# Two attention layers: phases of one and a half key tiles in place of steps of one

## The chip, the cores and the metric

The kernel runs on one core of a Trainium2 chip. The core has TensorE (PE), VectorE (DVE), ScalarE (ACT), GpSimd (POOL) and SyncE (SP); each takes its instructions in the order in which they were written, and semaphores hold an instruction back until what it needs is done. TensorE writes to PSUM, which has eight banks, each of 512 floats on 128 partitions; ScalarE and VectorE read it. The metric is the time of one execution on the device in microseconds (us); the median of several runs counts.

## The reference

Two layers, each normalizing an image of 4 x 256 x 64 x 64 floats by groups (_gn) and adding attention to it:

```python
q = jnp.einsum('oc,bchw->bohw', Wq, x).reshape(b, nh, hd, h * w)          # layer 0: 4096 queries,
k = lax.conv_general_dilated(x, Wk, window_strides=(SR, SR), ...)          # 1024 keys of a strided conv
attn = jnp.einsum('bhdn,bhdm->bhnm', q, k) + jnp.einsum('bhdn,hdm->bhnm', q, pos)
out = jnp.einsum('bhdm,bhnm->bhdn', v, jax.nn.softmax(attn * scale, axis=-1))

attn = jax.nn.softmax(jnp.einsum('bihd,bjhd->bhij', q, k) * scale, axis=-1) # layer 1: four areas of 1024 tokens
out = jnp.einsum('bhij,bjhd->bihd', attn, v) + _dwconv7(v_full, w_pe, b_pe)
return _conv1x1(out, w_proj, b_proj)
```

There are 8 heads of 32 channels; every query meets 1024 keys in either layer. All is float32.

## The kernel before

Work is cut into 8 blocks (layer A or B, image b), each of 16 units. A unit is 512 queries of four heads (one half of the channels), and has 8 key tiles of 128 keys: 1024 steps of one key tile in all. The main loop at the end of direct_path writes one step per pass, and the instruction order of all five engines is just the order of that writing (manual_schedule); no scheduler moves anything.

A step does the following.

- scores (L267): four products, one for each head, 32 channels deep, each in its own row tile of TensorE, into two pairs of PSUM banks (ps_pair, tag "s", three pairs that take turns). The first pair holds heads 0 and 1, the second heads 2 and 3.
- Two exponentials on ScalarE (L271), one for each pair, from PSUM into tiles p in SBUF (tag "p", ten buffers of 128 x 1024).
- weighted (L278): the values times the weights of the step before, four products, each in its own column tile, accumulated over the unit in the one bank av. At a unit's first step the finished av is copied to av_sb by ScalarE (L886), between the two exponentials.
- VectorE adds the p of each step to the first one of the unit (L865), one step later.
- do(g, j): whatever plan has for this step: loads, norms (ScalarE, L249), statistics, additions, transposes.
- Up to three parts of side tasks: the queue side holds the projections for q, k and v of later units, the output projections (product, L158) and the 7 x 7 convolution (L800). A part is four to eight products in column tiles. Most tasks have two parts, k and v of layer A four. A task's result lies in the one bank "side", from where ScalarE or VectorE moves it on.

Three steps after a unit's end come divisors (L288: ones times the summed weights, four products, in a pair of the tag "s") and divide: ScalarE copies the sums to den_sb (L305), POOL's queue takes them through DRAM to a narrow layout; five steps later reciprocals (L313) and their way back (L315, L317) to the tile rb, and five steps after that multiply (L320). So the PSUM banks are six for scores and divisors, one av, one side.

In the profile every float32 product appears as two matmuls, and a weight load (PEld) for each.

## Time and profile before

| What | us |
|---|---|
| median of 3 runs (3207.05 to 3210.25) | 3207.16 |
| span of the profiled execution | 3201.2 |
| scores, L267, busy, two blocks of layers | 601.5 + 593.8 |
| weighted sums, L278, busy | 552.5 + 545.2 |
| divisors, L288, busy | 142.4 |
| first score product starts at | 82.74 |
| last group of scores of the main loop starts at | 3174.61 |
| idle TensorE before a score product, all in all | 0.8 |

A line of groups has the source line, engine, operation, the tile written and those read, the shape and the count; then busy time, the mean of one in ns, and the idle time of the engine before them with what ended it. Matmuls overlap, and their ends are modelled; the starts are the better measure.

### The profile page before, as it was taken

Reading aid. Unit: us, or ns where it says so; the run is one execution under the profiler, and the core shown is the slowest. Engines: PE = TensorE matmul, PEld = TensorE weight load, DVE = VectorE, ACT = ScalarE, POOL = GpSimd, SP = SyncE. Lnnn points to the kernel's source line nnn. Section 1 sums busy time; section 2 is a strip of 40 time slices with the busy share of each in tenths; the row PEclk is TensorE's granted clock in tenths of the full one; section 3 lists DMA queues with packets and bytes.
Section 4 is the critical chain, followed back from the end, with each engine's and each line's share of the span. In section 5 each row is a group of like instructions: output and inputs, shape, how many; then the busy total and the mean of one; then the engine's idle time right before and its main releaser. Section 6 shows DMA issues by size and latency. Waiting matters only on the chain.

```text
span 3201.2 us, 75820 instructions
## 1 busy us (share of the span) xinstructions
PE 3159.5 (99%) x30762; PEld 960.0 (30%) x30762; DVE 2506.7 (78%) x2719; ACT 2520.7 (79%) x2988; POOL 487.7 (15%) x923
## 2 busy tenths in 40 slices
PE   7999999999999999999999999999999999999998
PEld 4233323332233332323223322323233333222222
DVE  3787897778887777877777777777788788888888
ACT  2888888887887878888887777777777777788876
POOL 0111121111211111111111111111111111111111
PEclk9999999999999999999999999999999999999999
DMA  5242343454545456777776666676555655423222
GB/s 183 43 104 74 92 105 85 95 125 108 129 111 140 125 135 173 163 175 177 198 175 161 182 174 158 169 176 161 155 143 144 167 151 149 128 72 80 70 51 59
DMA packets 648191, 421.53 MB, mean 132 GB/s; under 512 B 411773, under 2 KB 556637, under 8 KB 647833
## 3 DMA queue, kind: packets, MB, share of 16 engines
q1 hardware_dynamic: 619384, 380.11, 46.6%
q0 software_dynamic: 28448, 36.48, 4.6%
q8 instruction: 245, 4.01, 0.5%
q14 instruction: 114, 0.93, 0.1%
HBM read 318.32 MB, written 98.09 MB: 130 GB/s over the span
## 4 chain that ended last, share of the span: by engine, by line
PE 93%; issue 2%; DVE 2%; DMA 1%; ACT 1%; SPq 1%; POOL 0%; DVEq 0%; ACTq 0%; POOLq 0%
PE s L267 33%; PE av L278 29%; PE den L288 4%; PE k0ps L158 4%; PE q0ps L158 3%; PE k1ps L158 3%; PE q1ps L158 3%; PE v0ps L158 3%; PE conv_ps L800 3%; PE vals_ps L158 3%; PE ops L158 3%; DVE p L865 1%; ACT p L271 1%; DMA first<-in_x 0%; DMA share<-vals 0%
## 5 line engine op out<-in xcount | busy, mean ns | idle before, releaser
L865 DVE TENSOR_TENSOR p<-p 128x1024 f32<-128x1024 f32 x1790 | 2108.3, 1219 | 505.4 <-ACT p L271 454.9
L271 ACT ACTIVATE p<-s 128x1024 f32<-128x1024 f32 x2048 | 2016.6, 1026 | 512.7 <-PE s L267 497.3
L267 PE MATMUL s<-q,k_A 32*128 32x512 f32 x4096 | 601.5, 640 | 0.5 <-ACT p L271 0.3
L267 PE MATMUL s<-q,k_B 32*128 32x512 f32 x4096 | 593.8, 640 | 0.3 <-ACT p L271 0.3
L278 PE MATMUL av<-p,v_A 128*32 128x512 f32 x4096 | 552.5, 604 | 0.0
L278 PE MATMUL av<-p,v_B 128*32 128x512 f32 x4096 | 545.2, 603 | 0.0
L317 POOL DMA_DIRECT2D rb<-recs x508 | 252.0, 501 | 490.4 <-DMA recs<-few 414.5
L267 PEld LDWEIGHTS s<-q,k_B 32*128 32x128 f32 x4096 | 165.3, 182 | 384.5 <-issue 294.8
L267 PEld LDWEIGHTS s<-q,k_A 32*128 32x128 f32 x4096 | 172.8, 183 | 330.7 <-issue 253.1
L315 POOL DMA_DIRECT2D recs<-few x127 | 70.1, 552 | 1283.7 <-DVE sums L314 1208.4
L278 PEld LDWEIGHTS av<-p,v_A 128*32 128x32 f32 x4096 | 89.1, 108 | 381.2 <-issue 333.6
L278 PEld LDWEIGHTS av<-p,v_B 128*32 128x32 f32 x4096 | 87.6, 108 | 378.8 <-issue 335.2
L288 PE MATMUL den<-p,ones 128*32 128x512 f32 x1032 | 142.4, 606 | 3.1 <-DVE p L865 3.1
L307 POOL DMA_DIRECT2D few<-rows x127 | 72.3, 569 | 454.6 <-DMA rows<-den_sb 447.2
L158 PE MATMUL ops<-cv,wp_sb 128*32 128x512 f32 x1024 | 131.7, 593 | 4.4 <-DVE cv L577 3.0
L158 PE MATMUL k0ps<-taps,wkv 128*32 128x256 f32 x2048 | 130.2, 386 | 2.5 <-ACT taps L249 2.5
L158 PE MATMUL q1ps<-h,wqkv_sb 128*32 128x512 f32 x1024 | 131.5, 592 | 0.0
L158 PE MATMUL vals_ps<-hv,wqkv_sb 128*32 128x512 f32 x1024 | 129.9, 592 | 0.0
L306 POOL DMA_DIRECT2D rows<-den_sb x127 | 74.4, 586 | 363.6 <-ACT den_sb L305 358.6
L158 PE MATMUL k1ps<-h,wqkv_sb 128*32 128x512 f32 x1024 | 128.7, 592 | 0.2 <-ACT cout L811 0.2
L158 PE MATMUL q0ps<-hq,wq_sb 128*32 128x512 f32 x1024 | 128.2, 592 | 0.0
L158 PE MATMUL v0ps<-wkv,taps 128*32 128x256 f32 x2048 | 126.0, 379 | 0.3 <-ACT v_A L400 0.3
(90 smaller groups left out, 1686.3 us busy)
## 6 DMA issues: line engine op xcount, KB each, us to landing
rows<-vals SPq DMA_DIRECT2D x384, 195.9 KB
rb<-recs POOLq DMA_DIRECT2D x508, 64.0 KB, 3.3
share<-vals SPq DMA_DIRECT2D x128, 195.9 KB
vala<-vout SPq DMA_DIRECT2D x128, 144.0 KB
vals<-vout SPq DMA_DIRECT2D x128, 144.0 KB
vc<-vala SPq DMA_DIRECT2D x64, 288.0 KB
band<-mats SPq DMA_DIRECT2D x96, 176.0 KB
hq<-in_x SPq DMA_DIRECT2D x32, 512.0 KB
```

What stands on the lines that cost most here:

```text
L158: T.matmul(out[cols, :], lhsT=lhsT[:, cols], rhs=rhs, start=start, stop=stop)
L267: T.matmul(pairs[h // 2][:, h % 2, :], lhsT=k[rows, unit[0], j * P : (j + 1) * P], rhs=q[rows, :], start=True, stop=True,)
L271: exps = [lambda i=i: S.activation(p[i], pairs[i], AF.Exp, scale=SCALE) for i in range(2)]
L278: T.matmul(av[HD * h : HD * h + HD, :], lhsT=v[:, j, unit[0] * P + HD * h : unit[0] * P + HD * h + HD], rhs=p[h // 2][:, h % 2, :], start= ...
L288: T.matmul(dens[g][HD * h : HD * h + HD, :], lhsT=ones, rhs=p[h // 2][:, h % 2, :], start=(n == 0), stop=(n == len(ps) - 1),)
L306: G.dma_start(rows, den_sb[0:P:HD, :])
L307: G.dma_start(few[:, 0, :], rows.rearrange("h (q n) -> (h q) n", n=CH // HD))
L315: G.dma_start(recs.rearrange("h (q n) -> (h q) n", n=CH // HD), few[:, 1, :])
L317: G.dma_start(rb[HD * h : HD * h + HD, :], recs[h : h + 1, :].to_broadcast([HD, CH]))
L800: T.matmul(ps[HD * m : HD * m + HD, (2 * k + i) * size : (2 * k + i + 1) * size].rearrange("p (y x) -> p y x", y=NY), lhsT=band[:, half].r ...
L865: soon(1, lambda i=i: V.tensor_add(ps[0][i], ps[0][i], ps[j][i]))
```

## The change

A pass of the loop now is a phase of one and a half key tiles (683 phases for 1024 tiles). parts_of says which: an even phase has a whole key tile and the first half (256 queries) of the next one, an odd phase the second half and the whole tile after that. The scores of a phase fill all six banks: a has heads 0 and 2 of the whole tile, b heads 1 and 3, c the four halves, two to a bank. The halves of heads 1 and 3 go first, then the whole products of 0, 2, 1, 3, then, behind a fence, the halves of 0 and 2. In the next phase b and c have changed places. There are three exponentials in a phase, and the weighted sums of the phase before follow: four products of 512 columns and four of 256.

The weights of a unit are summed in a tile of their own, acc (two buffers of 128 x 2048): the first key tile's exponentials write it, the others are added to it. The buffers of tag "p" become six. den, and the two small products of a norm, move from the score banks to the side bank.

In the loop, when a unit ends inside a phase (cut), its last weighted sums come first, av is copied to av_sb between the second and the third exponential, and the new unit's weighted sums come last. Between the two stand either the divisors of a finished unit or up to two parts of one side task. After the weighted sums come further parts: up to four of one task if divisors were written, up to two if the task has more than two parts or more than seven parts wait. reciprocals stands at step 0 of the second unit on, four steps ahead of multiply.

```diff
-    first = [pool.tile([P, CT, CH], FP, tag="p", name=f"first_{c}", bufs=10) for c in range(NCH)]
+    first = [pool.tile([P, CT, CH], FP, tag="p", name=f"first_{c}", bufs=PB) for c in range(PB)]
+    rest_of_first = pool.tile([P, 4, CH], FP, tag="acc", name="first", bufs=2)
+    first += [rest_of_first[:, :2, :], rest_of_first[:, 2:, :]]
...
+    def ps_banks(n, name):
+        return psum.tile([P, 2, CH], FP, tag=f"s{n}", name=name, bufs=1)
+
+    turn = [0]
+
     def ps_pair(name):
-        return psum.tile([P, 2, CH], FP, tag="s", name=name, bufs=3)
+        turn[0] += 1
+        return ps_banks(turn[0] % 3, name)
...
-            ps = ps_pair(f"gm_{name}")[:, 0, :CT]
+            ps = ps_side(f"gm_{name}")[:, :CT]
...
+    HC = CH // 2
+    accs, made_p = {}, {}
+    in_bank, bank_count = tc.alloc_semaphore("in_bank"), [0]
+
+    def acc_of(g):
+        if g not in accs:
+            accs[g] = pool.tile([P, 4, CH], FP, tag="acc", name="acc", bufs=2)
+        return accs[g]
+
+    def pair_of(h):
+        return slice(2 * (h % 2), 2 * (h % 2) + 2)
+
+    def acc_half(g, u):
+        return acc_of(g).rearrange("p (l b) (u n) -> p u b l n", l=2, u=2)[:, u]
+
+    def parts_of(f):
+
+        full, half = (3 * f + 1) // 2, (3 * f // 2 + 1, 0) if f % 2 == 0 else (3 * f // 2, 1)
+        return (full if full < last else None), (half if half[0] < last else None)
+
+    def score_product(out, s, h, cols):
+        g, j = divmod(s, NKT)
+        rows, unit = slice(HD * h, HD * h + HD), units[g]
+        return T.matmul(
+            out, lhsT=unit[2]()[rows, unit[0], j * P : (j + 1) * P], rhs=unit[1]()[rows, cols], start=True, stop=True
+        )
+
+    def scores(f):
+
+        full, half = parts_of(f)
+        a, b, c = [ps_banks(n, "s") for n in ((0, 1, 2) if f % 2 == 0 else (0, 2, 1))]
+        every = slice(0, CH)
+
+        def half_product(h):
+
+            u = half[1]
+            return score_product(
+                c[:, h // 2, HC * (h % 2) : HC * (h % 2) + HC], half[0], h, slice(HC * u, HC * u + HC)
+            )
+
+        if half is not None:
+            for h in (1, 3):
+                first = half_product(h).then_inc(in_bank, 1)
+                tc.add_to_no_dep_group(f"first_{f}", first.ins)
+                tc.no_tile_sem_insts.add(first.ins.name)
+                bank_count[0] += 1
+        for h in (0, 2, 1, 3):
+            score_product((a, b)[h % 2][:, h // 2, :], full, h, every)
+        if half is not None:
+            fence = T.wait_ge(in_bank, bank_count[0])
+            tc.declare_fence(fence.ins, group=f"first_{f}")
+            for h in (0, 2):
+                half_product(h)
+
+        def exp_full(n):
+            g, j = divmod(full, NKT)
+            if j == 0:
+                p = acc_of(g)[:, pair_of(n), :]
+            else:
+                p = pool.tile([P, 2, CH], FP, tag="p", name="p", bufs=PB)
+            made_p[full, n] = p
+            S.activation(p, (a, b)[n], AF.Exp, scale=SCALE)
+
+        def exp_half():
+            if half is None:
+                return
+            (g, j), u = divmod(half[0], NKT), half[1]
+            if j == 0:
+                p = acc_half(g, u)
+            else:
+                p = pool.tile([P, 2, CH], FP, tag="p", name="p", bufs=PB).rearrange("p b (l n) -> p b l n", l=2)
+            made_p[half[0], 2 + u] = p
+            S.activation(p, c.rearrange("p b (l n) -> p b l n", l=2), AF.Exp, scale=SCALE)
+
+        return [lambda: exp_full(0), lambda: exp_full(1), exp_half]
+
+    def weighted(s, av, u=None):
+
+        g, j = divmod(s, NKT)
+        unit, v = units[g], units[g][3]()
         for h in range(4):
-            rows = slice(HD * h, HD * h + HD)
+            if u is None:
+                out, rhs = av[HD * h : HD * h + HD, :], made_p[s, h % 2][:, h // 2, :]
+            else:
+                out = av[HD * h : HD * h + HD, HC * u : HC * u + HC]
+                rhs = made_p[s, 2 + u][:, h // 2, h % 2, :]
             T.matmul(
-                pairs[h // 2][:, h % 2, :], lhsT=k[rows, unit[0], j * P : (j + 1) * P], rhs=q[rows, :],
-                start=True, stop=True,
+                out, lhsT=v[:, j, unit[0] * P + HD * h : unit[0] * P + HD * h + HD], rhs=rhs,
+                start=(j == 0 and not u), stop=(j == NKT - 1), skip_group_check=True,
             )
-        exps = [lambda i=i: S.activation(p[i], pairs[i], AF.Exp, scale=SCALE) for i in range(2)]
-        return p, exps
-
-    def weighted(unit, j, p, av):
-
-        v = unit[3]()
-        for h in range(4):
-            T.matmul(
-                av[HD * h : HD * h + HD, :], lhsT=v[:, j, unit[0] * P + HD * h : unit[0] * P + HD * h + HD],
-                rhs=p[h // 2][:, h % 2, :], start=(j == 0), stop=(j == NKT - 1),
-            )
-
-    def divisors(g, *ps):
-
-        dens[g] = ps_pair("den")[:, 0, :]
-        for n, p in enumerate(ps):
+
+    def add_up(s, n):
+
+        g = s // NKT
+        p, acc = made_p[s, n], acc_of(g)
+        to = acc[:, pair_of(n), :] if n < 2 else acc_half(g, n - 2)
+        V.tensor_add(to, to, p)
+
+    def divisors(g, *extra):
+
+        dens[g] = ps_side("den") if g < len(units) - 1 else ps_pair("den")[:, 0, :]
+        acc = accs.pop(g)
+        sets = [lambda h: acc[:, 2 * (h % 2) + h // 2, :]] + [lambda h: made_p[s, h % 2][:, h // 2, :] for s in extra]
+        for n, p in enumerate(sets):
             for h in range(4):
                 T.matmul(
-                    dens[g][HD * h : HD * h + HD, :], lhsT=ones, rhs=p[h // 2][:, h % 2, :],
-                    start=(n == 0), stop=(n == len(ps) - 1),
+                    dens[g][HD * h : HD * h + HD, :], lhsT=ones, rhs=p(h),
+                    start=(n == 0), stop=(n == len(sets) - 1),
                 )
 
     def divide(g, unit):
 
         if g == len(units) - 1:
 
-            rb = pool.tile([P, CH], FP, tag="p", name="rb", bufs=10)
+            rb = pool.tile([P, CH], FP, tag="p", name="rb", bufs=PB)
             V.reciprocal(rb, dens[g])
             V.tensor_mul(unit[4]()[:, unit[0], :], avs.pop(g), rb)
             spare.extend((dens.pop(g), rb))
@@ -319,7 +409,7 @@
         def multiply():
             V.tensor_mul(unit[4]()[:, unit[0], :], avs.pop(g), made["rb"])
 
-        at(g + 1, 7 if g < len(units) - 2 else 4, reciprocals)
+        at(*((g + 2, 0) if g < len(units) - 2 else (g + 1, 6)), reciprocals)
         at(g + 2, 4 if g < len(units) - 2 else 0, multiply)
...
+    final = len(units) - 1
+    av_of, weights_left, sums_left, opened = {}, {}, {}, set()
+    to_add, to_divide = deque(), deque()
+
+    def accumulate(s, u):
+
+        g = s // NKT
+        if g not in weights_left:
+            av_of[g] = psum.tile([P, CH], FP, tag="av", name="av", bufs=1)
+            weights_left[g] = 2 * NKT
+        weighted(s, av_of[g], u)
+        weights_left[g] -= 2 if u is None else 1
+        if weights_left[g] <= 2 * (NKT - 1):
+            opened.add(g)
+
+    def evict(g):
+        if weights_left[g] == 0 and g in av_of:
+            avs[g] = pool.tile([P, CH], FP, tag="av", name="av_sb", bufs=2)
+            S.copy(avs[g], av_of.pop(g))
+
+    def add_ready():
+
+        for _ in range(len(to_add)):
+            s, n = to_add.popleft()
+            g = s // NKT
+            if s % NKT and g not in opened:
+                to_add.append((s, n))
+                continue
+            if s % NKT and s != last - 1:
+                add_up(s, n)
+            sums_left[g] = sums_left.get(g, 2 * NKT) - 1
+            if sums_left[g] == 0:
+                to_divide.append(g)
+
+    def side_parts(budget):
+
+        mine, done = side[0] if side else None, 0
+        while done < budget and side and side[0] is mine:
+            advance()
+            done += 1
+
+    f = step = 0
+    before = []
+    while f < PHASES or before or plan or side or to_add or to_divide:
+        now[0] = step
+        exps = scores(f) if f < PHASES else [lambda: None] * 3
+        exps[0]()
+        due = bool(to_divide)
+        add_ready()
+        due = bool(to_divide) if f >= PHASES else due
+        cut = next((n for n in range(1, len(before)) if before[n][0] // NKT != before[0][0] // NKT), 0)
+        for s, u in before[:cut]:
+            accumulate(s, u)
+        exps[1]()
+        if cut:
+            evict(before[0][0] // NKT)
+        exps[2]()
+        while step < -(-3 * (f + 1) // 2):
+            do(*divmod(step, NKT))
+            step += 1
         waiting = sum(n for n, _ in side)
-        for n in range((waiting > 0) + (waiting > 7) + (waiting > 14) - (j == 2)):
-            if n and side[0] is not task_now:
-                break
-            task_now = side[0]
-            advance()
-            if not side:
-                break
-        before = None
-        if now[0] < last:
-            if j == 0:
-                av = psum.tile([P, CH], FP, tag="av", name="av", bufs=1)
-            sum_up(g, j, ps)
-            before = units[g], j, ps[j], av
-        now[0] += 1
+        whole = side[0][0] if side else 0
+        if due:
+            g = to_divide.popleft()
+            divisors(g, *([last - 1] if g == final else []))
+            if g < final:
+                divide(g, units[g])
+        else:
+            side_parts(2)
+        for s, u in before[cut:]:
+            accumulate(s, u)
+        add_ready()
+        if due:
+            side_parts(4)
+        elif whole > 2 or waiting > 7:
+            side_parts(2)
+        if before:
+            evict(before[-1][0] // NKT)
+        before = []
+        if f < PHASES:
+            full, half = parts_of(f)
+            before = sorted(([half] if half else []) + [(full, None)], key=lambda b: b[0])
+            to_add.extend((s, n) for s, u in before for n in ((0, 1) if u is None else (2 + u,)))
+        f += 1
```

More of the change, by code (lines that the diff above doesn't have):

```diff
@@ L47 @@
 LIMIT = 1e25
+PB = 6
 BLOCKS = [("A", b) for b in range(B)] + [("B", b) for b in range(B)]
 UNITS = 2 * NCH
+PHASES = -(-2 * len(BLOCKS) * UNITS * NKT // 3)
 @with_exitstack
@@ L229, in variances @@
         def variances():
-            ps = ps_pair(f"gv_{name}")[:, 0, :CT]
+            ps = ps_side(f"gv_{name}")[:, :CT]
             T.matmul(ps, lhsT=gmat, rhs=made["dev"], start=True, stop=True)
@@ L259, in v_tile @@
         return pool.tile([P, NKT, C], FP, tag="v", name="v_" + "_".join(map(str, key)), bufs=2)
-    def scores(unit, j):
-        q, k = unit[1](), unit[2]()
-        p = [pool.tile([P, 2, CH], FP, tag="p", name="p", bufs=10) for _ in range(2)]
-        pairs = [ps_pair("s"), ps_pair("s")]
-        for h in range(4):
-            rows = slice(HD * h, HD * h + HD)
+    HC = CH // 2
[5 more added lines that the diff above has]
+        return accs[g]
@@ L610, in project_last @@
                     )
-            within = pool.tile([P, 2 * len(units)], FP, tag="p", name="within", bufs=10)
+            within = pool.tile([P, 2 * len(units)], FP, tag="p", name="within", bufs=PB)
             V.tensor_scalar(within, sums.rearrange("p k g -> p (k g)"), LIMIT, None, ALU.is_le)
@@ L838, in direct_path @@
             plan_conv(b, n, (36, 58, 75.5, 93.5)[b] + (1.36, 1.06, 1.1, 1.1)[b] * n)
-    later = {}
-    def soon(steps, f):
-        later.setdefault(now[0] + steps, []).append(f)
     def do(g, j):
@@ L856, in direct_path @@
     )
-    def sum_up(g, j, ps):
-        if j == NKT - 1 and g == len(units) - 1:
-            soon(2, lambda: divisors(g, ps[0], ps[j]))
-            return
-        for i in range(2):
-            if j:
-                soon(1, lambda i=i: V.tensor_add(ps[0][i], ps[0][i], ps[j][i]))
-        if j == NKT - 1:
-            soon(3, lambda: divisors(g, ps[0]))
-            soon(3, lambda: divide(g, units[g]))
-    now[0] = 0
-    before = None
-    while now[0] < last or plan or later or side:
-        g, j = divmod(now[0], NKT)
-        if now[0] < last:
-            if j == 0:
-                ps = {}
-            ps[j], exps = scores(units[g], j)
-            exps[0]()
-        for f in later.pop(now[0], []):
-            f()
-        if before is not None:
-            weighted(*before)
-            if j == 0:
-                avs[g - 1] = pool.tile([P, CH], FP, tag="av", name="av_sb", bufs=2)
-                S.copy(avs[g - 1], before[3])
-        if now[0] < last:
-            exps[1]()
-        do(g, j)
-        waiting = sum(n for n, _ in side)
-        for n in range((waiting > 0) + (waiting > 7) + (waiting > 14) - (j == 2)):
-            if n and side[0] is not task_now:
-                break
-            task_now = side[0]
-            advance()
-            if not side:
-                break
-        before = None
-        if now[0] < last:
-            if j == 0:
-                av = psum.tile([P, CH], FP, tag="av", name="av", bufs=1)
-            sum_up(g, j, ps)
-            before = units[g], j, ps[j], av
-        now[0] += 1
```

## The prediction

> **What bounds the kernel now.** I read the page first, the busy table, then the chain, then the groups.
>
> ```profile
> PE 3159.5 (99%) x30762; PEld 960.0 (30%) x30762; DVE 2506.7 (78%) x2719; ACT 2520.7 (79%) x2988; POOL 487.7 (15%) x923
> ...
> PE 93%; issue 2%; DVE 2%; DMA 1%; ACT 1%; SPq 1%; POOL 0%; DVEq 0%; ACTq 0%; POOLq 0%
> ...
> L865 DVE TENSOR_TENSOR p<-p 128x1024 f32<-128x1024 f32 x1790 | 2108.3, 1219 | 505.4 <-ACT p L271 454.9
> L271 ACT ACTIVATE p<-s 128x1024 f32<-128x1024 f32 x2048 | 2016.6, 1026 | 512.7 <-PE s L267 497.3
> ```
>
> TensorE sets the end; VectorE and ScalarE have a fifth of the span free. Busy TensorE is not useful TensorE, so I took its timeline next, which gives the start of each group (start, length, engine, line, tile).
>
> ```profile
> 1530.98 1.14 PE L267 MATMUL s<-q,k_A 32*128 32x512 f32 x8
> 1532.05 1.07 PE L278 MATMUL av<-p,v_A 128*32 128x512 f32 x8
> 1532.93 1.06 PE L800 MATMUL conv_ps<-rows,band 88*32 88x128 f32 x32
> 1533.92 1.14 PE L267 MATMUL s<-q,k_A 32*128 32x512 f32 x8
> 1534.99 1.07 PE L288 MATMUL den<-p,ones 128*32 128x512 f32 x8
> 1535.88 1.04 PE L278 MATMUL av<-p,v_A 128*32 128x512 f32 x8
> 1536.85 1.14 PE L267 MATMUL s<-q,k_A 32*128 32x512 f32 x8
> ...
> 1545.90 1.90 PE L158 MATMUL q0ps<-hq,wq_sb 128*32 128x512 f32 x16
> 1547.73 1.14 PE L267 MATMUL s<-q,k_A 32*128 32x512 f32 x8
> ```
>
> From start to start: scores (S) 1.07, a weighted sum (AV) followed by another column-tiled group 0.88, the last column group before scores 0.97 (1535.88 to 1536.85). One part of a side task, as I call four side products, costs 1.83 - 0.97 = 0.86 (1545.90 to 1547.73 are two). Four products of 512 columns stream for 0.86; so a step pays 0.21 around S, 0.11 where column groups give way to scores, 0.03 entering AV: 0.35 in turning. A step without side work takes 2.07 and each part or divisor product adds 0.86.
>
> Last, a step where scores wait, and the timeline of ScalarE beside it.
>
> ```profile
> 411.97 1.31 PE L267 MATMUL s<-q,k_A 32*128 32x512 f32 x8
> 413.21 1.51 PE L278 MATMUL av<-p,v_A 128*32 128x512 f32 x8
> ```
>
> ```profile
> 411.07 1.02 ACT L271 ACTIVATE p<-s 128x1024 f32<-128x1024 f32 x1 [0.67 <-PE s L267]
> 412.10 0.58 ACT L886 COPY av_sb<-av 128x512 f32<-128x512 f32 x1
> 412.59 2.86 ACT L271 ACTIVATE p<-s 128x1024 f32<-128x1024 f32 x3
> ...
> 1529.23 1.02 ACT L271 ACTIVATE p<-s 128x1024 f32<-128x1024 f32 x1 [0.99 <-PE s L267]
> ```
>
> Three exponentials in 2.86 are one every 0.92. The copy put between two of them costs 0.59 more. The scores at 411.97 needed the bank that the exponential freed at 412.10, and their slot ended 1.11 after that: a wait on an exponential lets S end 1.13 behind it (I use the mean of several such steps). The scores of 1528.06 had streamed by 1529.02, and their exponential began at 1529.23: 0.2 from TensorE to ScalarE.
>
> **What the change takes away.** 1023 score groups become 682. A new phase has S of 1.07 + 0.43 = 1.50 and AV of 0.88 + 0.43 = 1.31, then 0.11: 2.93. Scores ran from 82.74 to 3174.61. In that stretch 1023 x 2.067 = 2115 becomes 682 x 2.93 = 1998: -116 us. Side products and divisors keep their number, hence 0.86 each. The 88 steps of before that hold nothing but S and AV lose about 0.2 each to waits like that at 411.97; that goes with them: -18 us.
>
> **The order inside S** decides whether 1.50 is right. Each head has its own row tile, and the heads' lengths differ: half, full, half, full. The four first matmuls of a group start within 0.02 us at 1530.98, and the second four 0.53 later, though in the program the two matmuls of one product stand next to each other: tiles proceed independently, so each row tile simply streams 1.28. The fence between (two semaphore increments, a wait, and four products queued behind it with all of AV) opens at 0.11 + 0.43 + 0.2 = 0.74 after the start of S; the products behind it are due at 0.11 + 0.86 = 0.97, less 0.11 of weight load. Hidden by 0.1; if the cover is gone, 0 to 0.1 for each phase, 0 to 68 us. I take 0.
>
> Against this stands the Trainium skill, "TensorE: Matmul & The Clock Gate", section "The mechanism": "MATMULs are pc-monotone in start AND end — strict FIFO, no reordering." By that rule, estimated with the same streams, S would need 3.0 us a phase, some 1000 us more in all; the trace's groups of four contradict it within one tiling, and I go by the trace.
>
> **What it adds: banks come free later.** Before, three pairs of banks rotate under two score halves of a step; now a phase fills all three (a, b, c), and the next phase needs c of this one for its full products of heads 1 and 3, and b for its first halves. Put S at 0: a is ready at 0.96, so exponentials begin at 1.15, 2.07, 2.99; b's ends at 3.10, c's at 4.02. The next S may start at 3.15 and cannot end before 4.02 + 1.13 = 5.15. In a phase with side work (2.93 + 2 x 0.86 = 4.65) nothing waits: the exponentials, the cover, lie under it. In a bare phase the next S should have ended at 2.93 + 1.50 = 4.43: 0.71 lost. Two in a row lose 0.94, three 1.43, four 1.65 (the start waits to 3.15 and 3.43 by turns).
>
> I counted phases in the changed program's TensorE order. A pass advances one task at most, so products come in lumps where before they came one a step:
>
> - 156 bare phases in 97 runs (52 of one, 34 of two, 8 of three, 3 of four): 37 + 32 + 11 + 5 = 85; 22 of the runs are followed by the next case, whose own wait swallows 0.49 each: 85 - 11 = +74. Norms that ScalarE does within runs overrun its 0.4 of idle time in some 24 places: +8.
> - 42 bare phases with a unit boundary. There the copy of av stands on ScalarE after the second exponential (2.99), ends at 3.58, and the new unit's AV, in the same single bank, starts at 3.63. TensorE was ready at 1.95 (after a half) or 2.39 (after a full product). The phase ends at 4.63 or 4.20, not 2.93: 1.48 x 42 = +62. In 43 others side work stands in that gap: 0.
> - 50 phases where divisors are followed by side products after AV. Divisors move from the score banks to the side bank, and the side products need den copied out. That copy stands on ScalarE behind the third exponential and the norms (0.25 on average): 3.91 + 0.25 + 0.59 + 0.05 = 4.80; TensorE is ready at 1.50 + 0.86 + 1.31 = 3.67: 1.12 x 50 = +56.
> - 77 with divisors alone (3.79), 260 with two parts, 53 with four: 0, covered by their own products.
>
> **VectorE.** Again 1790 additions, 598 of them with four runs of 256. Where one follows another into overlapping parts of the accumulator it starts 1.25 later instead of 1.14 (the dependent pair L383 and L384, medians 1222 and 1225 ns, starts 1.25 apart; independent additions 1.14): 598 x 0.12 = 72 us of VectorE, 2579 in all, under a longer span: off the path. What could show is its lag: a phase's exponentials reuse weights that VectorE must have added two phases before (six buffers, formerly ten), and the multiply that waits for rb stands four steps after the reciprocals in place of five. From reciprocals to rb's landing took 10.5 us at the median and over 12.9 in a quarter; four steps are about 12. VectorE waited 30 us there before; additions, and behind them ScalarE and S, queue behind it. Bounds 0 to 50 for all of this, by a wait of before of 3.06 that passed unseen by TensorE, and the 4 us that one den wait cost; I take +10. DMAs and POOL's issues keep count and order: 0.
>
> **Sum.** 3201.2 - 116 - 18 + 74 + 8 + 62 + 56 + 10 = 3277. The median of the runs lies 6 above the profiled span: 3283.
>
> **Rivals.**
>
> 1. Faster. The waits are smaller because exponentials begin earlier, or a bare phase's loss is made up in the next. Then the 116 + 18 stand against less than 134 of waits, i.e. under two thirds of my 200. For it: TensorE was starved less than 1% before at 79% of ScalarE. Against it: all three pairs are now in use at once, so a loaded neighbour cannot lend room. With no waits 3201 - 134 + 6 = 3073; with half of them 3173. Chance 0.22.
> 2. S is longer than 1.50, for the fence or because row tiles pair up (heads 1 and 3 first, then 0 and 2): 0.1 to 0.21 for each phase, 68 to 143 on top of the sum: 3350 to 3430. For it: all of AV is behind a wait in the queue. Against it: tiles ran independently. Chance 0.10.
> 3. VectorE binds in runs of bare phases: three additions, 3.5, beside 3.3 of period. It adds up to 60: 3340. Against it: it has 20% free and lag is bounded by two phases. Chance 0.08.
> 4. The phases are not formed as said: the order shows 682 score groups with three lengths, so no chance.
>
> **How the numbers follow.** My forecast, 3220 to 3345, has 0.55, with 3283 as its time; the first rival 0.22; the two others 0.18; 0.05 lies between the forecast and the first, at no change. Range 3165 to 3375: from half the waits to the longer S at its lower price, which leaves out about a tenth at each end. A measurement of this kernel tells about 0.2% from no change (6 us): faster 0.22, same 0.05, slower 0.73.
>
> **What would show it.** Score slots of 1.50 with side work before them, and up to 2.0 after a bare phase, waiting on the exponential; AV groups split by a wait on the av copy; side products waiting on the den copy for about a microsecond in 50 places; TensorE's idle share is up though its turns are a third fewer. Score slots all at 1.50 and no such waits would make the first rival right; 1.6 or more everywhere the second; VectorE without gaps in bare runs the third.

## The result and the profile after

| | before | after |
|---|---|---|
| median, us | 3208.03 (3207.05 to 3210.25) | 3467.07 (3463.21 to 3475.28) |
| ratio, 95% interval | | 1.0809 [1.0793, 1.0824] |
| span of the profiled execution, us | 3201.2 | 3465.9 |
| last group of scores of the main loop starts at | 3174.61 | 3432.42 |
| mean granted clock of TensorE | 0.998 | 0.977 |

Slower, as forecast, but by 259 us and not by 76: the time lies above the range. The page of the changed kernel: busy times, the chain of waits by engine, the two groups shown of before.

```profile
PE 3186.5 (92%) x36218; PEld 1394.4 (40%) x36218; DVE 2526.4 (73%) x2719; ACT 2468.6 (71%) x2988; POOL 486.1 (14%) x923
...
DVE 0%; PE 0%; DMA 0%; issue 0%; POOL 0%; DVEq 0%; POOLq 0%
...
L369 DVE TENSOR_TENSOR acc<-acc,p 128x1024 f32<-128x1024 f32 x1790 | 2123.7, 1220 | 716.7 <-PE av L359 322.5
L334 ACT ACTIVATE p<-s 128x1024 f32<-128x1024 f32 x1194 | 1162.2, 1026 | 479.8 <-PE s L296 445.0
```

No engine is full any more: TensorE fell from 99% to 92%, and VectorE and ScalarE are idler than before though they do the same work. The chain came out as its last steps alone (0% everywhere) and can't be used; so I read TensorE's timeline (start, length, engine, line, tile; in brackets the idle time and what ended it).

```profile
1370.48 1.07 PE L164 MATMUL q0ps<-hq,wq_sb 128*32 128x512 f32 x8
1373.76 1.27 PE L164 MATMUL q0ps<-hq,wq_sb 128*32 128x512 f32 x8 [2.21 <-ACT hq L261]
1374.78 2.81 PE L359 MATMUL av<-p,v_A 128*32 128x256 f32 x16
1377.52 1.75 PE L296 MATMUL s<-q,k_A 32*128 32x256 f32 x16
...
1503.08 1.59 PE L296 MATMUL s<-q,k_A 32*128 32x256 f32 x16
1504.60 1.50 PE L359 MATMUL av<-p,v_A 128*32 128x256 f32 x16
1506.26 2.04 PE L296 MATMUL s<-q,k_A 32*128 32x256 f32 x16 [0.17 <-ACT p L334]
1508.23 1.06 PE L359 MATMUL av<-p,v_A 128*32 128x512 f32 x8
1510.01 0.64 PE L359 MATMUL av<-acc,v_A 128*32 128x256 f32 x8 [0.71 <-ACT av_sb L961]
...
1513.41 1.04 PE L359 MATMUL av<-p,v_A 128*32 128x512 f32 x8
1515.84 1.92 PE L164 MATMUL vals_ps<-hv,wqkv_sb 128*32 128x512 f32 x16 [1.40 <-ACT den_sb L395]
...
1539.34 1.07 PE L164 MATMUL q0ps<-hq,wq_sb 128*32 128x512 f32 x8
1542.49 1.06 PE L164 MATMUL q0ps<-hq,wq_sb 128*32 128x512 f32 x8 [2.09 <-ACT hq L261]
```

Everything the forecast described is there: S takes 1.52 from start to start (1503.08 to 1504.60); after a bare phase it takes 1.97 and ends on the exponential (1506.26 to 1508.23); AV is split by the copy of av (1510.01); a side product waits 1.40 for den's copy (1515.84). What the forecast had at nothing is there too: the second part of a q projection waits 2.1 to 2.2 for its input hq, inside a phase with two parts. And after such a wait AV took 2.81 for what takes 1.47 elsewhere. ScalarE's timeline shows why hq is late.

```profile
1513.59 1.03 ACT L345 ACTIVATE p<-s 128x1024 f32<-128x1024 f32 x1
1514.49 0.82 ACT L261 ACTIVATE hv<-hv,norm_B 128x512 f32<-128x512 f32 x1
1515.20 0.59 ACT L395 COPY den_sb<-den 128x512 f32<-128x512 f32 x1
...
1538.89 1.94 ACT L334 ACTIVATE p<-s 128x1024 f32<-128x1024 f32 x2 [0.18 <-PE s L296]
1540.71 1.03 ACT L345 ACTIVATE p<-s 128x1024 f32<-128x1024 f32 x1
1541.62 0.82 ACT L261 ACTIVATE hq<-hq,norm_A 128x512 f32<-128x512 f32 x1
```

The norm of hq's second half is issued in the same phase as the product that reads it, behind all three exponentials of that phase. Of the 32 tiles hq ten make TensorE wait like this, 2.1 to 2.3 us each. In the kernel before none does: the norm of the second half ended at least 3.3 us ahead of the part that reads it. Where the forecast's lines show q0ps at 1545.90 (two parts in one step), that norm had ended at 1540.86:

```profile
1540.03 0.83 ACT L249 ACTIVATE hq<-hq,norm_A 128x512 f32<-128x512 f32 x1
```

To say where the time went, I took each step and each phase from the start of its scores to the start of the next, and subtracted the price of its products: 0.85 for four products of 512 columns, 0.5 for a norm's product, 0.36 for the turns. The price of all products fell from 3039 to 2915 us (-124; forecast -116). What exceeds it, the excess, rose from 52.5 to 434, where the forecast's terms make 52.5 - 18 + 74 + 8 + 62 + 56 + 10 = 244.5. The excess by kind of phase (the 43 phases in which a unit ends beside side work are counted with those of two and four parts):

| Phases | number | excess, us | forecast |
|---|---|---|---|
| scores and weighted sums alone | 198 | 143.9 | 74 + 8 + 62 = 144 |
| divisors and then side products | 50 | 67.1 | 56 |
| two parts | 296 | 132.2 | 0 |
| four parts | 60 | 50.6 | 0 |
| divisors alone | 77 | 40.1 | 0 |

Many phases of the last three rows did cost next to nothing: under 0.1 us of excess in 220 of the 296, 19 of the 60 and 60 of the 77. The median phase of two parts took 4.66 from start to start, where the forecast had 4.65. The excess sits in the others.

The waits by engine (total, times, longest) add VectorE's side, for the kernel before and then after:

```profile
DVE p L865 <- PE av L278: 48.2, 15, 11.8
DVE att_A L320 <- DMA rb<-recs: 25.4, 11, 6.8
```

```profile
DVE acc L369 <- PE av L359: 322.5, 87, 12.0
...
PEld s L296 <- ACT p L334: 133.2, 153, 4.4
...
PEld av L359 <- ACT av_sb L961: 89.1, 73, 2.1
...
DVE att_A L410 <- DMA rb<-recs: 70.7, 21, 9.6
...
PEld ops L164 <- DVE cv L667: 42.1, 23, 7.7
```

VectorE now stands 322 us until TensorE has read the first weights of a unit (they are the accumulator), and some of what it makes for TensorE comes late: cv above all, with 42 us.

Last, the granted clock. Its row in the page shows nine tenths or more in all of 40 slices but the last, which has eight, but the trace has 29 stretches of 3.41, 6.83 or 10.24 us (one of 18 at the end) at one half: 163 us, in 128 of which TensorE is busy. Before had two, with 3.4 busy. The window behind the wait at 1373.76 (columns: length, busy time of PE, PEld, DVE, ACT and POOL, clock, DMA share, GB/s):

```profile
1374.50:1377.90 3.40, 3.40 (x24) 1.04 (x20) 0.00 (x0) 0.59 (x1) 1.44 (x3) 0.50 1.03 233
```

TensorE works there without a gap at half its clock; so 128 busy us cost up to 64, of which 62 lie ahead of the last scores.

### The profile page after: what moved, and what is told of

Same layout as the page of the kernel before. It is cut to its first block, busy times and chain, and to the rows that moved or that the text cites. A ratio compares the mean times of both kernels' runs of the same rounds, so it can differ in the third digit from the quotient of the medians.

```text
span 3465.9 us, 87567 instructions
## 1 busy us (share of the span) xinstructions
PE 3186.5 (92%) x36218; PEld 1394.4 (40%) x36218; DVE 2526.4 (73%) x2719; ACT 2468.6 (71%) x2988; POOL 486.1 (14%) x923
## 5 line engine op out<-in xcount | busy, mean ns | idle before, releaser
L369 DVE TENSOR_TENSOR acc<-acc,p 128x1024 f32<-128x1024 f32 x1790 | 2123.7, 1220 | 716.7 <-PE av L359 322.5
L334 ACT ACTIVATE p<-s 128x1024 f32<-128x1024 f32 x1194 | 1162.2, 1026 | 479.8 <-PE s L296 445.0
L345 ACT ACTIVATE p<-s 128x1024 f32<-128x1024 f32 x598 | 619.6, 1036 | 8.2 <-DVE acc L369 4.3
L296 PE MATMUL s<-q,k_A 32*128 32x256 f32 (+1 forms) x5464 | 591.7, 520 | 22.4 <-ACT p L334 17.9
L296 PE MATMUL s<-q,k_B 32*128 32x256 f32 (+1 forms) x5456 | 569.8, 513 | 12.5 <-ACT p L334 11.7
L359 PE MATMUL av<-p,v_A 128*32 128x256 f32 (+1 forms) x4784 | 473.6, 503 | 0.0
L296 PEld LDWEIGHTS s<-q,k_A 32*128 32x128 f32 x5464 | 327.3, 186 | 332.8 <-issue 89.1
L296 PEld LDWEIGHTS s<-q,k_B 32*128 32x128 f32 x5456 | 332.8, 184 | 312.6 <-issue 87.5
L359 PE MATMUL av<-p,v_B 128*32 128x512 f32 (+1 forms) x4776 | 453.6, 490 | 0.0
L334 ACT ACTIVATE acc<-s 128x1024 f32<-128x1024 f32 x172 | 167.2, 1025 | 109.3 <-PE s L296 109.3
L378 PE MATMUL den<-acc,ones 128*32 128x512 f32 x1024 | 150.0, 627 | 25.9 <-DVE acc L369 12.9
```

Source lines behind the costliest of these rows:

```text
L296: return T.matmul(out, lhsT=unit[2]()[rows, unit[0], j * P : (j + 1) * P], rhs=unit[1]()[rows, cols], start=True, stop=True)
L334: S.activation(p, (a, b)[n], AF.Exp, scale=SCALE)
L345: S.activation(p, c.rearrange("p b (l n) -> p b l n", l=2), AF.Exp, scale=SCALE)
L359: T.matmul(out, lhsT=v[:, j, unit[0] * P + HD * h : unit[0] * P + HD * h + HD], rhs=rhs, start=(j == 0 and not u), stop=(j == NKT - 1), sk ...
L369: V.tensor_add(to, to, p)
L378: T.matmul(dens[g][HD * h : HD * h + HD, :], lhsT=ones, rhs=p(h), start=(n == 0), stop=(n == len(sets) - 1),)
```

## The experiments

Edits are to the changed kernel unless another one is named. "Excess" is the sum explained above, "half" the time that TensorE was busy at half its clock; half of its fall is the most that the clock can have in a gain. The medians of the kernel before beside these runs lie between 3204 and 3210, so differences between runs hold to some 5 us.

| Run | median, us | ratio to before | excess | half |
|---|---|---|---|---|
| changed kernel | 3467.07 | 1.0809 [1.0793, 1.0824] | 434 | 128 |
| e1 | 3358.02 | 1.0466 [1.0448, 1.0484] | 331 | 56 |
| e2 | 3416.83 | 1.0655 [1.0637, 1.0673] | 382 | 82 |
| e3 | 3400.53 | 1.0599 [1.0581, 1.0616] | 368 | 107 |
| e4 | 3345.06 | 1.0412 [1.0380, 1.0445] | 312 | 136 |
| e5 | 3425.16 | 1.0676 [1.0658, 1.0694] | 398 | 100 |
| e6 | 3459.99 | 1.0775 [1.0750, 1.0801] | 427 | 113 |
| e7 | 3295.99 | 1.0279 [1.0262, 1.0296] | 265 | 89 |
| e8 | 3287.80 | 1.0240 [1.0217, 1.0263] | 261 | 84 |
| e9 | 3187.55 | 0.9945 [0.9928, 0.9962] | 157 | 45 |
| e10 | 3236.58 | 1.0098 [1.0081, 1.0114] | 200 | 54 |
| e11 | 3216.71 | 1.0031 [1.0022, 1.0041] | 183 | 44 |
| e12 | 3182.16 | 0.9929 [0.9916, 0.9943] | 159 | 32 |
| e13, of before | 3195.65 | 0.9969 [0.9956, 0.9982] | 48 | 6 |
| e14, of before | 3203.62 | 0.9997 [0.9987, 1.0006] | 50 | 3 |
| e15 | 3439.72 | 1.0731 [1.0717, 1.0746] | | 76 |

### The suspects one by one

**e1**

```diff
-        V.tensor_add(to, to, p)
```

> Leaves out VectorE's additions of the softmax weights (the divisors then hold the first key tile alone); TensorE, ScalarE and the order of everything else stay. Theory A (TensorE stands in its own queue behind ScalarE's copies, norms and exponentials of the same phase; VectorE's lag is a minor part): only the waits that name VectorE go (cv 28, den's sums 18, xm 14, mv 15 us of the changed kernel) and a part of the exponentials' own, 50 to 110 us less, 3357 to 3417. Theory B (VectorE, with six weight buffers and one accumulator, lags and everything else waits for it): 200 us less or more, near or under the time of before (3208).

109 us faster. The excess of phases with two parts fell from 132 to 78, that of bare ones only from 144 to 132. The waits of e1:

```profile
PEld s L296 <- ACT p L334: 133.2, 158, 1.7
...
PEld av L359 <- ACT av_sb L960: 90.7, 74, 2.1
...
PEld ops L164 <- DVE cv L666: 5.3, 1, 5.3
```

Scores and AV wait as long as with additions: these waits belong to ScalarE. The output projection's wait for cv went from 42 to 5.

**e2**

```diff
-                at(g - 2, 1 + 2 * t, lambda c=c, t=t: norm_chunk(c, t))
+                at(g - 2, t, lambda c=c, t=t: norm_chunk(c, t))
...
-            at(g, j + 2, lambda c=c: soon_tasks([(2, project, c, to) for to in range(CT)]))
+            at(g, j + 4, lambda c=c: soon_tasks([(2, project, c, to) for to in range(CT)]))
...
-            at(0, when + 5 + t, lambda t=t: norm(t))
+            at(0, when + 2 + t, lambda t=t: norm(t))
...
-            plan_values(b, c, (17.8, 42, 54.5, 67)[b] + (2.0, 1.5, 1.3, 2.2)[b] * c)
+            plan_values(b, c, (18.3, 42, 54.5, 67)[b] + (2.0, 1.5, 1.3, 2.2)[b] * c)
```

The last line begins the first image's values half a unit later.

> The norms of hq and hv stand two or three steps sooner, the output projections two steps later, so that a side product's input is no longer made in the phase that multiplies it. Theory A: the waits of side products on hq, hv and cv (25, 22 and 28 us) shrink to a third, 40 to 75 us less, 3392 to 3427. Theory B: those waits are only where the lag shows; less than 20 us.

50 us faster; phases with two parts (269 in place of 296) exceed their work by 67 instead of 132 us, and the waits on hq and hv are gone. One to three key tiles more between an input and its product were enough. The order of the phases changed with it: bare phases and those with side products after divisors are 22 and 20 more, and exceed their work by some 36 us more.

**e3**

```diff
-        if due:
-            side_parts(4)
-        elif whole > 2 or waiting > 7:
+        if not due and (whole > 2 or waiting > 7):
```

> No side products follow the divisors in a phase (none needs the side bank before den is copied out); their parts go to other phases, by the instruction order 164 phases with scores and weighted sums alone in place of 198. Theory A: the 60 us of waits on den_sb go, and 34 bare phases fewer at 0.73 us save 25: 60 to 100 us less, 3367 to 3407. Theory B: within 20 us of the changed kernel.

67 us faster; the excess that ends on den's copy fell from 60 to 9. Part of the gain has another source: there are 34 bare phases fewer, and what bare phases exceed fell from 144 to 126. The forecast's 56 was this mechanism at nearly its size.

**e4**

```diff
-            side_parts(2)
+            side_parts(1 + (waiting > 4 or cut > 0))
...
-        if due:
-            side_parts(4)
-        elif whole > 2 or waiting > 7:
+        if not due and waiting > 10:
```

Also a task begun is finished ahead of divisors and norm products, as these need its bank.

> Side tasks are advanced by one part a phase (two when more than four parts wait or a unit ends in the phase) in place of two or four: by the instruction order 32 phases with scores and weighted sums alone in place of 198, 25 with side products after the divisors in place of 50. Theory A: exponential waits 109 to about 30, av copy waits 55 to about 10, den copy waits 60 to 30: 110 to 170 us less, 3297 to 3357. Theory B: the same work on VectorE in less time, so less than 40 us. A third theory (C: score phases themselves are too long, by the fence and the short products) expects no change from any of the four but the first.

122 us faster. Only 32 bare phases are left. A new wait came: 51 us of excess for the side bank that VectorE has to empty (xm).

**e5**

```diff
-        at(*((g + 2, 0) if g < len(units) - 2 else (g + 1, 6)), reciprocals)
+        at(*((g + 1, 7) if g < len(units) - 2 else (g + 1, 6)), reciprocals)
```

> Only the reciprocals go back to step 7 of the unit before (five steps ahead of the multiply, as before the change). VectorE waited 103 us on rb in the changed kernel, 28 before. Theory A1 (the 109 us that VectorE's lag costs, by the run without additions, come in good part from VectorE standing on rb, with additions and cv behind it): rb waits fall to 40 us or less and the time by 20 to 50 us, 3417 to 3447. Theory B1 (the lag comes from additions that stand on the new unit's first weighted sum, 323 us against 48 before, and from the smaller number of buffers): rb waits fall alike, the time by less than 15 us.

42 us faster: the five steps of before instead of four. VectorE's waits on rb fell from 103 to 28 us. The forecast had 0 to 50 for the whole of VectorE's lag.

**e6**

```diff
-        at(g, j + 1, means)
-        at(g, j + 3, variances)
+        apart = key != ("A", 0)
+        at(g, j + 1 + apart, means)
+        at(g, j + 3 + 2 * apart, variances)
```

The first image's values begin half a unit later here too.

> The two small products of each group norm stand two and four steps, in place of one and two, behind what feeds them (not for the first image); the first image's values start half a unit later. Theory A (a product in the phase that makes its input stops TensorE's queue): the waits on mv, gvar and gmean (15, 12 and 3 us) mostly go: 15 to 35 us less, 3432 to 3452. Theory B: less than 10 us.

A miss: 7 us, within the noise. TensorE's idle time that ends on a step of a norm is 19 us, against 24 in the changed kernel: the norm's product stands elsewhere, but still ahead of a side product that needs its bank (e12 comes back to this).

### All of them, and what was left

**e7** joins the edits of e2, e4, e5 and e6; a task begun is also finished in the phase before divisors, and the first image's values begin another 0.4 of a unit later.

> Everything at once on the changed kernel: side parts one by one with no side products after divisors and no unfinished task at a divisor, norms sooner, projections later, norm products apart, reciprocals sooner. Bare phases 31 in place of 198. Theory A: the parts add up to some 60 to 80% of their sum (122 + 50 + 25 + 30 + 30 = 257): 3200 to 3310, and the lower end needs VectorE's lag gone too. Theory C (the phases themselves cost more than steps): it stays above 3320.

171 us faster, where the four one by one make 221. The largest excess left is on xm, 67 us.

**e8** adds to e7

```diff
-        exps[1]()
         if cut:
             evict(before[0][0] // NKT)
+        exps[1]()
```

> As e7, and where a unit ends within a phase, av is copied out ahead of the second exponential in place of the third: the copy can start 0.8 us sooner, the second and third exponential 0.6 later. With side work between the two weighted sums in 81 of 85 such phases there is little to gain: within 15 us of e7. More than 25 us less would mean that the copy still holds the new unit's weighted sums and VectorE's first additions behind them.

8 us. The waits on the output projection and TensorE's timeline show what stands in the way then:

```profile
PEld ops L164 <- DVE xm L692: 69.0, 28, 5.7
```

```profile
1860.47 1.92 PE L164 MATMUL ops<-cv,wp_sb 128*32 128x512 f32 x16
1862.21 1.47 PE L369 MATMUL av<-p,v_B 128*32 128x256 f32 x16
1868.50 3.23 PE L164 MATMUL ops<-cv,wp_sb 128*32 128x512 f32 x16 [4.82 <-DVE xm L692]
```

The second output projection waits 4.82 until VectorE has taken the first out of the one side bank, and then runs slowly: 3.23 for what took 1.92.

**e9** is e8 without the line removed in e1.

> e8's kernel without VectorE's additions of p to the running sum of softmax weights (left out: the sums hold the first block alone, so outputs differ from the reference). Theory V: what keeps e8 above the kernel before (3287.8 against about 3209) is VectorE's lag, which shows as the waits on xm and acc. Then this run is 60 to 110 us faster than e8: 3180 to 3230. Rival X: the wait on xm is for the turn of the projection's bank itself, whoever evicts it, and the rest is the exponential's wait; then less than 40 us is gained, and it stays over 3247.

100 us: what kept e8 above the kernel before goes with VectorE's additions. Like is compared with like in e13 below, the kernel before without its additions (3195.65): e9 is 8 us ahead of that.

**e10** is e8 with

```diff
-            V.scalar_tensor_tensor(x_to, by_column(ps), bproj_sb[:, to : to + 1], x_to, ALU.add, ALU.add)
+            moved = pool.tile([P, CH], FP, tag="cout", name=f"moved_{b}_{c}_{to}", bufs=2)
+            S.activation(moved, ps, AF.Identity, bias=bproj_sb[:, to : to + 1])
+            V.tensor_add(x_to, x_to, by_column(moved))
```

> e8's kernel with the projection's sums moved out of PSUM by ScalarE (with the bias), so that the side bank no longer waits for VectorE; VectorE adds them to x from SBUF. Theory V: the 62 us of waits on xm fall below 20 and the time by 30 to 60: 3228 to 3258. Rival X (the bank waits for whoever evicts it, and ScalarE stands behind its exponentials): the wait moves from xm to the new tile, and the time stays within 20 us of e8's 3287.8.

51 us. The projection's wait for its bank, 69 us in e8, is 16 us here:

```profile
PEld ops L164 <- ACT moved L693: 15.6, 17, 2.1
```

VectorE still waits 284 to 300 us for AV in e10, e11 and e12.

**e11** adds to e10: the memsets of the values' borders are issued two or three key tiles ahead of the values' tasks, in place of inside them.

> e10 with the values' border memsets issued some phases sooner, away from the values' evictions. Theory V: the 23 us of waits on vout fall by half or more and the time by 10 to 25 against e10. Rival: the values wait for the eviction of their own products, not for the memsets, and the time stays within 6 us of e10.

20 us. Now the steps of the norms, and the side products behind them as in e6, were the largest kind of wait left: 23 us of TensorE's idle time. TensorE in e11:

```profile
1313.27 1.59 PE L306 MATMUL s<-q,k_A 32*128 32x256 f32 x16
1314.79 0.38 PE L252 MATMUL gv_B<-dev_B,gmat 128*128 128x2 f32 x2
1317.52 3.08 PE L164 MATMUL vals_ps<-hv,wqkv_sb 128*32 128x512 f32 x16 [2.35 <-ACT gvar_B L253]
```

**e12** adds to e11

```diff
-        at(g, j + 1 + apart, means)
-        at(g, j + 3 + 2 * apart, variances)
+        soon = (lambda f: f()) if key in (("A", 0), ("A", 1)) else behind.append
+        at(g, j + 1 + apart, lambda: soon(means))
+        at(g, j + 3 + 2 * apart, lambda: soon(variances))
...
+        while behind:
+            behind.pop(0)()
         if before:
             evict(before[-1][0] // NKT)
```

and begins the second sample's values 2 to 3 key tiles later.

> e11's kernel with the products of the group norm (gm, gv) issued as a phase's last work instead of ahead of its side products, and the second sample's values begun 2 to 3 key tiles later, behind the load that held them. Theory V (what is left above the kernel before is a side product that stands behind VectorE and ScalarE in the same phase): in e11 eight phases with a norm product ahead of a side product exceed their work by some 3 to 4 us each beyond the mean, and one waits 7 us for its load, 20 to 35 us together; the time falls from 3216.7 to 3182 to 3197, below the kernel before. Rival: these waits move to the next phase, since the ScalarE copy stands behind the exponentials there too; then less than 10 us is gained and the time stays at 3207 or more.

It is below the kernel before: 0.9929 [0.9916, 0.9943], 22 us or 0.7%. TensorE's idle time on steps of the norms fell from 23 us to 5. The same product (gv_B of that norm), and the page's busy times:

```profile
1293.70 1.47 PE L370 MATMUL av<-p,v_A 128*32 128x512 f32 x16
1294.99 1.04 PE L164 MATMUL q0ps<-hq,wq_sb 128*32 128x512 f32 x8
1296.73 0.38 PE L252 MATMUL gv_B<-dev_B,gmat 128*128 128x2 f32 x2 [0.70 <-ACT q L536]
1297.05 1.59 PE L307 MATMUL s<-q,k_A 32*128 32x256 f32 x16
```

```profile
PE 3090.3 (97%) x36218; PEld 1414.5 (44%) x36218; DVE 2515.9 (79%) x2719; ACT 2497.2 (78%) x3050; POOL 489.3 (15%) x923
```

The norm's product now lies between AV and the next scores, where nothing follows that needs its bank until the scores are through, 1.5 us later (1297.05 to 1298.56).

### Prices of the phases, or of any kernel here?

**e13** is the kernel before without its additions (L865).

> The kernel before without VectorE's additions of p to the running sum of softmax weights (left out: the divisors come from the first key tile alone, so outputs differ from the reference). It tells whether the 109 us that leaving them out gave in the changed kernel (e1) are a price of the phases. Theory P: they are, and before VectorE's work is hidden: this run is within 15 us of the kernel before. Rival Q: VectorE costs the kernel before as much; then it is 40 us or more faster than before.

8 us by the medians (0.9969). TensorE is as full as it was with them:

```profile
PE 3158.0 (99%) x30762; PEld 961.7 (30%) x30762; DVE 456.1 (14%) x929; ACT 2500.4 (78%) x2988; POOL 481.1 (15%) x923
```

Before hides 2100 us of additions for 8; of e1's 109, some 100 are a price of the phases.

**e14** is the kernel before with e10's edit.

> The kernel before with the projection's sums moved out of PSUM by ScalarE and added to x from SBUF, as e10 does it in the changed kernel, where it was worth about 51 us. Theory P: the wait for the side bank is a price of VectorE's lag in the phases, and the kernel before gains less than 10 us or loses as much. Rival Q: it gains 20 us or more, and the comparison of e12 with the kernel before would credit the phases with what this edit gives to any of the two.

No change (0.9997): e10's 51 us were given to the phases alone, and e12's lead does not come from that edit.

**e15** is the changed kernel with

```diff
+        for _ in range(FILL[kind].get(begun[kind] - 1, 0)):
+            for i in range(4):
+                T.matmul(
+                    ps[HD * i : HD * i + HD, :], lhsT=nothing,
+                    rhs=wqkv_sb[:, 0, :2, :].rearrange("p k o -> p (k o)"), start=False, stop=False,
+                )
```

ahead of the second half of 15 side products; nothing is a tile of zeros.

> The changed kernel with products of zero weights (added to the bank of the side task, without effect on its sum) put into 15 of its waits: ten of q's projections that stand 2.4 us before their second half and five of the values' that stand 2.2 to 6.5 us, with two products groups of 0.86 us each in the short ones, three in one of 3.0 and six in the two long ones, always less than the wait. Nothing else is changed, and no wait is shortened by it. In the changed kernel's trace the granted clock is at one half in 29 stretches, 163 us together, 128 of them with TensorE busy; eight of the stretches follow these 15 waits, 3.4 us each after four of q's and 3.4, 6.8, 6.8 and 3.4 after the values', 34 together. Theory K: the waits cost a second time, since TensorE streams at half speed after them; with TensorE kept busy most of these stretches are gone and the time falls by 8 to 17 us, and the record shows some 20 stretches. Rival N: the lower clock costs nothing that another wait does not hide; the time stays within 4 us of 3467.

27 us faster, more than either theory had. TensorE at the place shown of the changed kernel at 1370:

```profile
1357.40 1.07 PE L178 MATMUL q0ps<-hq,wq_sb 128*32 128x512 f32 x8
1358.28 1.90 PE L164 MATMUL q0ps<-wqkv_sb,nothing 128*32 128x512 f32 x16
1360.67 1.06 PE L178 MATMUL q0ps<-hq,wq_sb 128*32 128x512 f32 x8 [0.49 <-ACT hq L275]
1361.56 1.47 PE L373 MATMUL av<-p,v_A 128*32 128x256 f32 x16
```

The second half starts 3.27 after the first, as before the edit (3.28), so the wait is no shorter (12 of the 15 are as long as before within 0.02 us, and so are all 15 together); but AV behind it takes 1.47 instead of 2.81. Half-clock stretches fell from 29 to 17 and TensorE's busy time in them from 128 to 76; half of these 52 is 26, about what was gained. Of the 12 stretches that are gone eight stood at the filled waits: all that stood there. Product by product against the changed kernel's trace, e15 gains 15 us at the filled waits, as theory K has it. Most of the other 10 are gained where nothing was edited, at stretches that e15 does not have (near 98, 480, 832 and 1869 in the changed kernel) or has shorter (1975); why they went stays open.

## Why the forecast was right in direction and wrong in size

- **Fewer turns, -116:** right; -124 by the prices above, and phases of two parts without a wait took 4.66 where 4.65 was forecast. e12 does the same products in phases and collects a part of it, so the idea was not empty.
- **S of 1.50, fence at nothing:** right; 1.51 to 1.52 where nothing holds it. The heads' different lengths do run side by side. The sentence on strict order that the forecast quoted from the Trainium skill ("TensorE: Matmul & The Clock Gate", section "The mechanism") would have made it 3.0 by the forecast's estimate; the measurement decides against it here.
- **Bare phases, 74 + 8 + 62:** right, 143.9 for 144, and e1, where they are 132, shows that they are not VectorE's: the rows name ScalarE. The 42 at a unit's end exceed by 66 (forecast 62), the others by 78 (82). What brings it down is having fewer bare phases: e4 left 32, with the projections spread.
- **Divisors then side products, 56:** right in mechanism; 67 in the trace, most of it on den's copy (60 in all, 9 in e3). So the direction was no luck: the waits that the forecast named came to 211 where it had 200.
- **"77 with divisors alone (3.79), 260 with two parts, 53 with four: 0, covered by their own products":** this step failed: 223 us. The cover was counted against the score banks alone. A side product has inputs of its own, and the phase brought two parts together and put three exponentials ahead of the norm that feeds the second one. In these phases TensorE stood idle 62 us for hq, hv and cv (e2, which gives these inputs more time, was worth 50), 16 for steps of the norms, 11 for the sums ahead of divisors, 20 for exponentials, and the lower clock below took up to 53. A side product also has a bank of its own, which VectorE or ScalarE must empty before the next one. In the changed kernel that was small (8 us of idle time on xm in these phases); it became the largest wait once the parts were spread (e10: 51, e12: some 33 by the ratios, with the later values).
- **VectorE, +10 with bounds 0 to 50:** mis-sized; about 100 (e1 less e13), overlapping the term above, and up to 36 of it by way of the clock (busy at half 128 before e1's edit, 56 after it). The shorter time from the reciprocals to rb alone cost 42 (e5). The bound came from two single waits of the kernel before, which say little about what a late VectorE costs in the phases.
- **Not in the forecast: the clock.** Many of the waits of 2 us and more which these two terms make go with a clock of one half for 3.4 us or a multiple of it: up to 62 of the 434, 53 of it in the phases put at nothing, 6 in the bare ones, whose waits are all under 1.7 but one. Of the changed kernel's waits of 2.4 us and more all 17 go with such a stretch, of those from 2.0 to 2.4 eight of 15, of those from 0.5 to 2.0 six of 117. e15, which fills 15 waits without shortening them in all, shows that the waits cause it. On the multiple of 3.41 the trace agrees with the Trainium skill, "TensorE: Matmul & The Clock Gate", section "What's actually happening", which gives a free-running window of that length; but four of ten waits of 2.2 us on hq, shorter than a window, were followed by a stretch.
- **The sum:** the excess is 189.5 above the forecast's (223 and 11 more in the rows of the table, less the 34.5 of the steps of before and the 10 of VectorE that the forecast had besides), the turns gave 8 more, and the end after the last scores is 7 longer (33.4 against 26.6): 3277 + 189 = 3466, the profiled span. The median lies 1 above that span, not 6.
- **Rivals:** "VectorE binds" had the right engine, but not by its throughput (it is idle more than before): its lateness costs. "Faster" needed waits under two thirds of 200; they were some 400 (434 less 34.5). "S is longer" is out: 1.52. e12 shows that the phases can be faster once side work is placed for them.

What stays open: the first addition of a unit waits for TensorE to have read the accumulator. Adding out of place would show what that is worth; it wasn't tried, nor were seven or eight weight buffers, so which part of VectorE's 100 us the six buffers have is not shown.

## What to carry to other kernels

When steps are merged, list for each piece of side work its input, its bank and who makes or empties each, and ask again whether that maker, now behind more work of the same pass, is in time; a phase with spare products is not covered if the spare product itself is late. Time gained by fewer turns on the full engine is real, but it comes with larger lumps on its helpers: spread the lumps first. And price a wait of two microseconds on TensorE at more than its length: the clock may halve behind it.

## What the runs showed of the hardware that was not expected

TensorE's waits of 2 us and more can cost a second time, at half the clock, though a wait is shorter than the stretch of 3.41 us that follows it. Products of zero weights, put into ten waits of 2.1 to 2.3 us and five of 2.0 to 6.3, left these waits as long in all and made the kernel 27 us faster, some 15 of it at the waits themselves. The page's row of clocks hides all but the last of these stretches in slices of 87 us; the mean shows them (0.977 against 0.998).
